# The next image's first q products held in PSUM during a feed-forward, and three smaller moves, in a two-layer attention kernel

## The chip, the cores and the metric

The kernel runs on one core of one Trainium2 chip, as one program. The metric is the device time of one execution in microseconds (us); a kernel's time is the median of its runs. The core's engines each work through an instruction queue of their own in order: TensorE (PE in the profile; PEld are its weight loads), VectorE (DVE), ScalarE (ACT), GpSimd (POOL) and SyncE (SP, which here only issues DMA transfers). They wait for each other through semaphores. Products of PE land in PSUM[...]. The instructions' order within an engine and their waits are laid by a scheduler (the `tile` library) from the Python program; a buffer is taken from a pool, and one that takes the place of an older one waits until that is no longer read.

## The reference

Eight images of 32 x 32 tokens (T = 1024) with C = 384 channels go through two layers, each added to its input. Layer 0 is a group norm and an attention of six heads with a bias from relative positions; layer 1 is a norm and causal attention of one head, and then a norm and a feed-forward with weights cut to signs and activations scaled by their largest absolute value.

```python
# layer 0
qkv = _gn(x).reshape(b, hw, c) @ qkv_w + qkv_b          # -> q, k, v: [48, 1024, 64]
attn = einsum('bqd,bkd->bqk', q * SCALE, k)
rel_h = einsum('bhwc,hkc->bhwk', r_q, Rh); rel_w = einsum('bhwc,wkc->bhwk', r_q, Rw)   # r_q is q, by row and column
attn = softmax(attn + rel_h[..., :, None] + rel_w[..., None, :])
x = x + (attn @ v) @ proj_w + proj_b
# layer 1, attention
t = _ln_t(x);  q, k, v = t @ Wq, t @ Wk, t @ Wv
x = x + softmax(causal(q @ k.T * C ** -0.5)) @ v
# layer 1, feed-forward: sign-cut weights by five groups, activations scaled by absmax per image;
# the groups take in five of eight images: for the other three this part is zero
h = gelu(_bitlinear(_ln_t(x), W1, b1), approximate=False)
x = x + _bitlinear(h, W2, b2)
```

## The kernel before

The kernel works through the images one after the other. PSUM is one pool of eight banks of 128x512 fp32 (`o_tile`); SBUF tiles of 128x1024 are `page` (12 of them), those of 128x3080 `image` or `flat` (11).

The group norm of the next image is made between the value products and the scores of layer 1's attention. Its two small products (mean and variance over the groups, "gmean" and "gvar") each wait for VectorE, and are waited for by it:

```python
def group_norm_T(b, xT=None):
    xT = load_T(b) if xT is None else xT
    ...                                    # bn_stats, bn_aggr -> mv
    nc.tensor.matmul(ps[:, 0:1], over_group, mv[:, 0:1], start=True, stop=True)     # gmean
    nc.vector.tensor_copy(cs[:, 0:1], ps[:, 0:1])
    nc.vector.tensor_tensor(d[:, 0:1], mv[:, 0:1], cs[:, 0:1], ALU.subtract)
    nc.vector.scalar_tensor_tensor(d[:, 1:2], d[:, 0:1], d[:, 0:1], mv[:, 1:2], ALU.mult, ALU.add)
    ps = pools.o_tile(f"gvar_{b}")
    nc.tensor.matmul(ps[:, 0:1], over_group, d[:, 1:2], start=True, stop=True)      # gvar
    ...                                    # sqrt on ScalarE, reciprocal, xT normalized in place
    return xT
```

Layer 0 of an image begins with q and k: for each m (0 to 2 are q of the head pairs, 3 to 5 their k) six products of 128x512. From q come the bias tables ("rel"), which go through DRAM to be laid out anew ("far", "near") and are then split in a rounded part and its rest ("hi" and "lo", by `place`), and sent to the r tiles, hi by SP's queue and lo by POOL's. `place(0, ...)` runs ahead of the bursts; pairs 1 and 2 are fetched step by step from the generator `later`.

```python
def queries_keys(m):
    for half in range(2):
        ps = pools.o_tile(f"qk_{b}_{m}_{half}")
        for i in range(NC):
            nc.tensor.matmul(ps, wqkv_sb[:, i, ts(m, P)], xT[:, i, t], start=(i == 0), stop=(i == NC - 1))
        ...                                # evacuated with the bias added, half 0 by ScalarE, half 1 by VectorE
def place(p, near, pages):
    for d in range(2):
        nc.scalar.copy(hi, src)
        nc.vector.tensor_tensor(lo, src, hi.bitcast(F32), ALU.subtract)
        if d == 0: yield
    for part in range(4):
        for d in range(2):
            for i in range(2):
                (nc.gpsimd if i else nc.sync).dma_start(out=r[part][:, p, :]..., in_=pages[i]...)
for m in range(2 * NPAIR):
    queries_keys(m)
    if 0 < m <= NPAIR:
        near.append(positions(m - 1))      # the rel products, far, near
...                                        # v; place(0) as a whole
if pools.fast and b == 0:
    join_biases(pools)
    multiply_out(pools)                    # wqk = wq @ wk.T * C ** -0.5, once, from wqT and wkT
```

The attention of layer 0 runs in bursts of units. A unit is one block of 128 keys (c) against one half of the queries; its two heads are two products of q and k and two of the unit matrix and r, added in PSUM, and two exponentials. The value products of a burst come behind the scores of the next. `residual` loads x and adds the output bias to it on POOL, eight additions.

```python
for p in range(NPAIR):
    for n, burst in enumerate(bursts):     # 2, 3, 3, 3, 3, 2 units
        prs = [scores(p, *u) for u in burst]
        for u in pending:
            values(*u)
        if n == 0:
            if p > 0: few = set_aside(p - 1, *last)
            elif b > 0: xt = residual()
            avs = ...
        if b == 0 and xt is None and next(signs[0]):   # image 0: a step of the sign-cutting of the weights
            xt = residual()
        if p == 0 and n > 0:
            with tc.issue_after(last_exp[0]):
                next(later, None)          # a step of place for pairs 1 and 2
        ...
```

The feed-forward: a norm in two halves, each with four groups of three transposes ("pt"), twenty-four tiles of the first GEMM (y1) with two evacuations each, the largest absolute value over everything, and only then gelu and the second GEMM (y2).

```python
def ffn(xt, b):
    for half in range(2):
        rs = layer_norm_T(xt, xs[0], half, f"2_{b}", xs[1])
    ...                                    # 24 x 6 products y1, ScalarE evacuates, VectorE takes maxima
    s, _ = absmax_scale(...)               # partition_all_reduce on POOL
    for j in range(NJ):
        ...                                # gelu to hi and lo; 24 products y2; VectorE evacuates
```

Of the kernel before, what the change touches and what calls it, by code (L numbers as in the profile page):

```python
# [17 lines left out]
P = 128  # L18
B, H, W, C = 8, 32, 32, 384
T = H * W  # L20
NJ = T // P
NC = C // P
# [9 lines left out]
B_FFN = NG * GSB  # L32
# [41 lines left out]
def conv_attn_hybrid(  # L74
# [19 lines left out]
    nc = tc.nc  # L94
# [15 lines left out]
    wqkv_sb, wproj_sb, wv_sb = (tile_of(n, [P, NC, w]) for n, w in (("wqkv_sb", 3 * C), ("wproj_sb", C), ("wv_sb", C)))  # L110
# [30 lines left out]
    ident = const.tile([P, P], F32, name="ident")  # L141
# [146 lines left out]

    def stages(pools):

        def transpose_tiles(dst, srcs, engine):

            n = len(srcs)
            pt = pools.o_tile("pt")
            for i, s in enumerate(srcs):
                nc.tensor.transpose(pt[:, ts(i, P)], s, ident)  # L296
            engine(dst, pt[:, : n * P].rearrange("p (i q) -> p i q", i=n))

        def load_T(b):
# [7 lines left out]
        def group_norm_T(b, xT=None):  # L307

            xT = load_T(b) if xT is None else xT
            st = pools.small.tile([P, NC, 2, 6], F32, tag="gst", bufs=2, name=f"gst_{b}")  # L310
            mv = pools.small.tile([P, 2], F32, tag="gmv", name=f"gmv_{b}")
            for k in range(NC):
                for half in range(2):
                    nc.vector.bn_stats(st[:, k, half, :], xT[:, k, ts(half, 512)])
            nc.vector.bn_aggr(mv, st.rearrange("p k a s -> p (k a s)"))

            ps = pools.o_tile(f"gmean_{b}")
            nc.tensor.matmul(ps[:, 0:1], over_group, mv[:, 0:1], start=True, stop=True)
            cs = pools.small.tile([P, 2], F32, tag="gcs", name=f"gcs_{b}")
            nc.vector.tensor_copy(cs[:, 0:1], ps[:, 0:1])  # L320
            d = pools.small.tile([P, 2], F32, tag="gd", name=f"gd_{b}")
            nc.vector.tensor_tensor(d[:, 0:1], mv[:, 0:1], cs[:, 0:1], ALU.subtract)
            nc.vector.scalar_tensor_tensor(d[:, 1:2], d[:, 0:1], d[:, 0:1], mv[:, 1:2], ALU.mult, ALU.add)
            ps = pools.o_tile(f"gvar_{b}")
            nc.tensor.matmul(ps[:, 0:1], over_group, d[:, 1:2], start=True, stop=True)
            nc.vector.tensor_scalar_add(d[:, 0:1], ps[:, 0:1], 1e-5)
            nc.scalar.activation(d[:, 0:1], d[:, 0:1], AF.Sqrt)
            nc.vector.reciprocal(cs[:, 1:2], d[:, 0:1])
            for k in range(NC):
                nc.vector.tensor_scalar(  # L330
                    xT[:, k, :], xT[:, k, :], cs[:, 0:1], cs[:, 1:2], ALU.subtract, ALU.mult
                )
            return xT

        def layer_norm_T(xt, xT, half, name, xlo=None):

# [73 lines left out]
            nc.vector.tensor_reduce(seen[:, 1, i : i + 1], reciprocal, AX.X, ALU.add)  # L410


        def layer0(b, xT):


# [7 lines left out]
            def queries_keys(m):  # L423
                p = m % NPAIR
                bias = bqk[:, m : m + 1]
                for half in range(2):
                    t = ts(half, 512)
                    ps = pools.o_tile(f"qk_{b}_{m}_{half}")
                    for i in range(NC):
                        nc.tensor.matmul(  # L430
                            ps, wqkv_sb[:, i, ts(m, P)], xT[:, i, t], start=(i == 0), stop=(i == NC - 1)
                        )
                    if m < NPAIR:
                        dst = q[:, p, t]
                    else:
                        dst = k[:, p, t].rearrange("d (g n i) -> d g i n", n=2, i=P)
                        ps = ps.rearrange("d (g i n) -> d g i n", n=2, i=P)
                    if half:
                        nc.vector.tensor_scalar_add(dst, ps, bias)
                    else:  # L440
                        nc.scalar.activation(dst, ps, AF.Identity, bias=bias)
# [92 lines left out]
                pass  # L534
            if pools.fast and b == 0:
                join_biases(pools)
                multiply_out(pools)

            def residual():
                xt = load_x(pools, b)  # L540
# [6 lines left out]
        def attend0_fast(residual, b, q, k, r, v, later):  # L547
# [84 lines left out]
            xt = None  # L632
# [6 lines left out]
            for p in range(NPAIR):  # L639
                sums = [pools.page(f"sum0_{b}_{p}_{half}") for half in range(2)]  # L640
                for n, burst in enumerate(bursts):
                    prs = [scores(p, *u) for u in burst]
                    for u in pending:
                        values(*u)
                    if n == 0:
                        if p > 0:
                            few = set_aside(p - 1, *last)
                        elif b > 0:
                            xt = residual()
                        avs = [pools.o_tile(f"av0_{b}_{p}_{half}") for half in range(2)]  # L650
                    if b == 0 and xt is None and next(signs[0]):
                        xt = residual()
                    if p == 0 and n > 0:
                        with tc.issue_after(last_exp[0]):
                            next(later, None)
                    if n == 2 and p > 0:
                        divide(p - 1, few)
                    pending = [(p, *u, pr, sums, avs) for u, pr in zip(burst, prs)]
                last = (sums, avs)
# [71 lines left out]
        def attention1(xt, more, b, between):  # L731
# [29 lines left out]
            for j in range(4, NJ):  # L761
                values(j)

            got = between()
            (attend1_fast if pools.fast else attend1_general)(xt, b, q, xT, v)
            return got

        def attend1_fast(xt, b, q, xT, v):

            room = [pools.flat(f"pr1_{b}_{i}") for i in range(2)]  # L770
            tot = pools.small.tile([P, NJ], F32, tag="tot1", name=f"tot1_{b}")
# [29 lines left out]
            prs = []  # L801
            for c in range(NJ):
                prs.append(scores(c))
                for work in signs:
                    next(work, None)
                if c >= 2:
                    values(c - 2)
# [4 lines left out]
            values(NJ - 1)  # L812
            check(tot, rt, b * (NPAIR + 1) + NPAIR)

        def attend1_general(xt, b, q, xT, v):
            mask = pools.work.tile([P, P], F32, tag="mask", name=f"mask_{b}")
            make_causal_mask(nc, mask, mask_val=MASKED)

# [50 lines left out]
            w2m = [a2[:, ts(i, C)] for i in range(8)] + [rest[:, half + i * C : half + (i + 1) * C] for i in range(4)]  # L869
            return w1k, w2m  # L870

        def ffn(xt, b):
            xs = [pools.halves(f"{n}_{b}", F32R) for n in ("lnT_2", "lnlo_2")]
            for half in range(2):
                rs = layer_norm_T(xt, xs[0], half, f"2_{b}", xs[1])

            early = pools.small.tile([P, 1], F32, tag="early", name=f"early_{b}")
            nc.scalar.activation(early, rs[:, 0:1], AF.Gelu)
# [7 lines left out]
            for half in range(2):  # L886
                for m in range(NM):
# [10 lines left out]
                    if m + 1 in cuts:  # L898
                        n = cuts.index(m + 1)
                        for i in (2 * half, 2 * half + 1):  # L900
                            nc.vector.tensor_reduce(  # L901
                                am[:, i, n - 1 : n], pairs[i][:, cuts[n - 1] : cuts[n], :, :], AX.XYZ, ALU.max, apply_absolute_value=True
                            )
            s, _ = absmax_scale(am.rearrange("p i n -> p (i n)"), f"1_{b}")

# [42 lines left out]
        def run(pools):  # L950
            gn = load_T(0)
            if pools.fast:
                load_weights(pools)
            gn = group_norm_T(0, gn)
            if pools.fast:
                make_unit(pools)
            for b in range(B):
                xt, more = layer0(b, gn)

                def between():  # L960

                    g = group_norm_T(b + 1) if b + 1 < B else None
                    return g

                gn = attention1(xt, more, b, between)
                add = ffn(xt, b) if b < B_FFN else None

                def finish(b=b, xt=xt, add=add):
                    if add:
# [59 lines left out]
```

## Time and profile before

| | |
|---|---|
| Time, median of three runs | 2508.88 us (2507.89 to 2511.79) |
| Span of the profiled execution | 2506.5 us |
| PE clock granted, mean | 0.988 |
| POOL, busy | 300.4 us, 12% |
| q and k products of layer 0 (L430) | 256.9 us, 576 products |
| variance product of image 1's group norm (L325) | begins at 243.11 us, 1.05 us of waiting before it |
| image 0's first feed-forward | from its transposes at 290 us to layer 0 of image 1 at 373.76 us |

The profile's busy share counts an engine as at work from an instruction's start to its modelled end; a PE that is "busy" may still run at half its clock. PEclk in the windows of the trace is the clock that PE was granted, 1.00 being full. A wait is put down to the releaser that came last. Line numbers (L430) are those of the kernel before. A name such as f_qk is the buffer, with f_ for the path of the kernel that runs.

Three stretches of image 0 and 1 around the change, from the windows of the trace (columns: window, length, busy us and instructions of PE, PEld, DVE, ACT, POOL, then PEclk, DMA share, GB/s):

```profile
294.00:296.00 2.00, 0.00 (x0) 0.00 (x0) 0.73 (x2) 1.95 (x4) 0.00 (x0) 0.75 0.00 0
296.00:298.00 2.00, 1.45 (x7) 1.45 (x8) 1.74 (x4) 1.75 (x3) 0.00 (x0) 0.50 0.00 0
298.00:300.00 2.00, 2.00 (x9) 1.84 (x8) 1.75 (x4) 1.44 (x3) 0.00 (x0) 0.50 0.00 0
340.00:342.00 2.00, 2.00 (x8) 2.00 (x7) 0.76 (x2) 1.97 (x3) 0.00 (x0) 0.50 0.00 0
```

They are the end of the second norm, the first products of the feed-forward, and the first products of the second GEMM.

### The profile page before, as it was taken

To read this page: it belongs to the slowest core of one execution; us is meant where nothing else is said; L and a number is where in the kernel's file an instruction comes from. 1 tells how busy PE (TensorE), PEld (TensorE's weight loads), DVE (VectorE), ACT (ScalarE), POOL (GpSimd) and SP (SyncE) were. 2 spreads that over 40 slices of the span, in tenths; PEclk is the share of its full clock that TensorE was granted. 3 is DMA by queue.
4 is the path that set the end of the run, shared out by engine and by line. 5 is a ranking of instruction groups with operands and counts; after the bars stand their busy time and mean duration, and the time that the engine had idled before them with its cause. 6 is when DMAs were issued, how large, how long until landed. Compare 5 with 4: busy or idle time off the path is not lost.

```text
span 2506.5 us, 25716 instructions
## 1 busy us (share of the span) xinstructions
PE 2405.9 (96%) x9378; PEld 1296.8 (52%) x9378; DVE 1416.6 (57%) x2182; ACT 1016.2 (41%) x1742; POOL 300.4 (12%) x389
## 2 busy tenths in 40 slices
PE   7899999999899999999999999989999999999998
PEld 3335684345764456743458544567435543554344
DVE  4696553963556744548645577345585248524852
ACT  3451363631645413645227354145551155114520
POOL 1120002300014000022000230001300031002200
PEclk9999999999999999999999999999999999999999
DMA  7632207211036101082110541011810172007100
GB/s 160 199 119 75 76 1 159 68 64 38 1 86 142 51 13 38 1 179 61 52 38 1 118 109 51 13 38 45 161 48 1 45 144 64 1 26 157 46 0 27
DMA packets 154792, 169.97 MB, mean 68 GB/s; under 512 B 113408, under 2 KB 126048, under 8 KB 153120
## 3 DMA queue, kind: packets, MB, share of 16 engines
q1 hardware_dynamic: 134416, 98.93, 16.9%
q0 software_dynamic: 17184, 69.22, 9.5%
q8 instruction: 77, 1.26, 0.2%
q10 hardware_dynamic: 3056, 0.08, 0.1%
q14 instruction: 59, 0.48, 0.1%
HBM read 75.38 MB, written 42.47 MB: 47 GB/s over the span
## 4 chain that ended last, share of the span: by engine, by line
PE 93%; DVE 2%; DMA 2%; ACT 1%; POOL 1%; issue 1%; SPq 0%; ACTq 0%; DVEq 0%
PE f_s L559 14%; PE f_av L580 14%; PE f_qk L430 10%; PE f_av L794 7%; PE f_s L781 7%; PE f_y L929 7%; PE f_y L890 7%; PE f_v L368 5%; PE f_q L739 5%; PE f_v L507 4%; PE f_s L563 4%; PE f_pj L368 2%; PE f_rel L457 2%; PE f_pj L669 2%; PE f_pt L296 1%; PE f_pj L674 1%
## 5 line engine op out<-in xcount | busy, mean ns | idle before, releaser
L569 ACT ACTIVATE f_pr<-f_s 128x512 f32<-128x512 f32 x768 | 408.5, 597 | 351.5 <-PE f_s L563 294.3
L559 PE MATMUL f_s<-f_q,f_k 64*128 64x512 f32 x1536 | 412.6, 608 | 6.3 <-ACT f_pr L569 6.3
L577 DVE TENSOR_TENSOR f_sum<-f_sum,f_pr 128x1024 f32<-128x1024 f32 x288 | 373.6, 1347 | 17.5 <-ACT f_pr L569 17.0
L580 PE MATMUL f_av<-f_pr,f_v 128*64 128x512 f32 x1536 | 359.6, 601 | 0.0
L563 PE MATMUL f_s<-f_r,unit 64*128 64x512 f32 x768 | 305.8, 767 | 7.8 <-issue 6.7
L430 PE MATMUL f_qk<-f_gnT,wqkv_sb 128*128 128x512 f32 x576 | 256.9, 600 | 2.0 <-DVE f_gnT L330 2.0
L559 PEld LDWEIGHTS f_s<-f_q,f_k 64*128 64x128 f32 x1536 | 145.6, 186 | 173.7 <-issue 98.7
L580 PEld LDWEIGHTS f_av<-f_pr,f_v 128*64 128x64 f32 x1536 | 98.2, 136 | 217.8 <-issue 194.7
L794 PE MATMUL f_av<-f_v,f_pr 128*128 128x385 f32 x576 | 194.5, 486 | 0.0
L781 PE MATMUL f_s<-f_q,f_lnT 128*128 128x512 f32 (+3 forms) x576 | 194.4, 487 | 0.0
L430 PEld LDWEIGHTS f_qk<-f_gnT,wqkv_sb 128*128 128x128 f32 x576 | 108.1, 191 | 144.2 <-issue 131.4
L495 POOL DMA_DIRECT2D f_r<-f_far x192 | 101.8, 533 | 438.8 <-DVE f_far L488 398.1
L794 PEld LDWEIGHTS f_av<-f_v,f_pr 128*128 128x128 f32 x576 | 108.7, 190 | 78.5 <-issue 11.5
L781 PEld LDWEIGHTS f_s<-f_q,f_lnT 128*128 128x128 f32 x576 | 102.6, 190 | 81.0 <-issue 57.4
L788 ACT ACTIVATE f_pr<-f_s 128x512 f32<-128x512 f32 (+3 forms) x96 | 47.1, 490 | 208.8 <-DVE f_s L786 154.3
L563 PEld LDWEIGHTS f_s<-f_r,unit 64*128 64x128 f32 x768 | 79.1, 187 | 101.2 <-issue 99.2
L894 ACT ACTIVATE f_h<-f_y,b_sb 128x256 f32<-128x256 f32 x240 | 99.6, 472 | 72.8 <-PE f_y L890 72.8
L901 DVE TENSOR_REDUCE am<-f_h 128x1 f32<-128x1024 f32 (+2 forms) x80 | 71.6, 946 | 101.5 <-ACT f_h L894 101.5
L739 PE MATMUL f_q<-f_lnT,wqk 128*128 128x512 f32 x288 | 127.5, 592 | 0.0
L368 PE MATMUL f_v<-wv_sb,f_lnT 128*128 128x384 f32 x384 | 126.5, 486 | 0.0
L507 PE MATMUL f_v<-wqkv_sb,f_gnT 128*128 128x384 f32 x384 | 125.1, 486 | 0.0
L542 POOL TENSOR_TENSOR f_x<-f_x,pb 128x384 f32<-128x384 f32 x64 | 117.9, 1871 | 10.0 <-issue 9.7
(161 smaller groups left out, 3015.2 us busy)
## 6 DMA issues: line engine op xcount, KB each, us to landing
f_far<-f_far SPq DMA_DIRECT2D x48, 512.0 KB, 5.2
f_r<-f_far POOLq DMA_DIRECT2D x192, 128.0 KB, 4.1
f_r<-f_far SPq DMA_DIRECT2D x192, 128.0 KB, 2.8
f_gnT<-in_xT SPq DMA_DIRECT2D x24, 512.0 KB, 4.7
f_x<-in_x SPq DMA_DIRECT2D x32, 384.0 KB, 5.4
out_y<-f_x POOLq DMA_DIRECT2D x28, 384.0 KB, 4.3
f_near<-f_far SPq DMA_DIRECT2D x128, 64.0 KB, 4.6
f_w1a<-w1s POOLq DMA_DIRECT2D x5, 1536.0 KB, 6.7
```

Of the source, the lines that this page charges most:

```text
L368: nc.tensor.matmul(ps[:, :C], xT[:, k, ts(j, P)], w[:, k, cols], start=(k == 0), stop=(k == NC - 1))
L430: nc.tensor.matmul(ps, wqkv_sb[:, i, ts(m, P)], xT[:, i, t], start=(i == 0), stop=(i == NC - 1))
L507: nc.tensor.matmul(ps, keys[:, i, j // 2, j % 2], wqkv_sb[:, i, 2 * C :], start=(i == 0), stop=(i == NC - 1))
L559: nc.tensor.matmul(sc[par], k[rows[par], p, ts(c, P)], q[rows[par], p, ts(half, 512)], start=True, stop=False)
L563: nc.tensor.matmul(sc[par], unit[rows[par], c // 2 % 2].rearrange("i h w -> i (h w)"), r[2 * (c // 4) + c % 2][rows[par], p, ts(half, 512) ...
L569: last_exp[0] = nc.scalar.activation(pr[:, ts(par, 512)], sc[par], AF.Exp).ins
L577: nc.vector.tensor_tensor(sums[half], prev, pr, ALU.add)
L580: nc.tensor.matmul(avs[half][ts(par, HD), :], v[:, c, ts(h, HD)], pr[:, ts(par, 512)], start=(c == 0), stop=(c == NJ - 1),)
L739: nc.tensor.matmul(ps, wqk[:, k, ts(m, P)], xT[:, half, k, :], start=(k == 0), stop=(k == NC - 1))
L781: nc.tensor.matmul(sc[:, lo:], xT[:, c // 4, k, ts(c % 4, P)], q[:, half, k, lo:], start=(k == 0), stop=(k == NC - 1),)
L794: nc.tensor.matmul(av[:, : C + 1], prs[c][:, ts(j - c, P)], v[:, c, :], start=(c == 0), stop=(c == j))
L890: nc.tensor.matmul(ps, w1k[i // 2][:, ts(m, P)], xs[i % 2][:, half, i // 2, :], start=(i == 0), stop=(i == 2 * NC - 1))
```

## The change

Four parts, none of which changes what is computed.

1. The q products of layer 0 are split from their evacuation (`project_qk`). While image b's feed-forward runs (images 0 to 4), those of image b + 1 for m = 0 are put behind the last transpose of the norm's first half, and those for m = 1 behind the maximum, ahead of the second GEMM. They stay in PSUM, two banks each, until layer 0's `queries_keys` takes them from the dictionary `ahead` and evacuates them; the scheduler may place the evacuation earlier, as soon as the products are done.
2. `group_norm_T` becomes a generator that pauses before the variance product; it goes on behind the first scores of layer 1's attention.
3. The steps of `place` for pairs 1 and 2 begin with the first burst (`p == 0`) and not the second (`p == 0 and n > 0`), to have r in time for pair 1.
4. `multiply_out`, once a kernel, moves from the place ahead of the bursts to image 0's second burst, so that PE needn't wait there for its two weight loads.

```diff
@@ -288,12 +288,14 @@
 
     def stages(pools):
 
+        last_transpose = [None]
+
         def transpose_tiles(dst, srcs, engine):
 
             n = len(srcs)
             pt = pools.o_tile("pt")
             for i, s in enumerate(srcs):
-                nc.tensor.transpose(pt[:, ts(i, P)], s, ident)
+                last_transpose[0] = nc.tensor.transpose(pt[:, ts(i, P)], s, ident).ins
             engine(dst, pt[:, : n * P].rearrange("p (i q) -> p i q", i=n))
 
         def load_T(b):
@@ -321,6 +323,7 @@
             d = pools.small.tile([P, 2], F32, tag="gd", name=f"gd_{b}")
             nc.vector.tensor_tensor(d[:, 0:1], mv[:, 0:1], cs[:, 0:1], ALU.subtract)
             nc.vector.scalar_tensor_tensor(d[:, 1:2], d[:, 0:1], d[:, 0:1], mv[:, 1:2], ALU.mult, ALU.add)
+            yield xT
             ps = pools.o_tile(f"gvar_{b}")
             nc.tensor.matmul(ps[:, 0:1], over_group, d[:, 1:2], start=True, stop=True)
             nc.vector.tensor_scalar_add(d[:, 0:1], ps[:, 0:1], 1e-5)
@@ -330,7 +333,6 @@
                 nc.vector.tensor_scalar(
                     xT[:, k, :], xT[:, k, :], cs[:, 0:1], cs[:, 1:2], ALU.subtract, ALU.mult
                 )
-            return xT
 
         def layer_norm_T(xt, xT, half, name, xlo=None):
@@ -410,6 +412,18 @@
             nc.vector.tensor_reduce(seen[:, 1, i : i + 1], reciprocal, AX.X, ALU.add)
 
 
+        ahead = {}
+
+        def project_qk(b, xT, m):
+
+            made = [pools.o_tile(f"qk_{b}_{m}_{half}") for half in range(2)]
+            for half in range(2):
+                for i in range(NC):
+                    nc.tensor.matmul(
+                        made[half], wqkv_sb[:, i, ts(m, P)], xT[:, i, ts(half, 512)], start=(i == 0), stop=(i == NC - 1)
+                    )
+            return made
+
         def layer0(b, xT):
@@ -423,13 +437,9 @@
             def queries_keys(m):
                 p = m % NPAIR
                 bias = bqk[:, m : m + 1]
-                for half in range(2):
+                made = ahead.pop((b, m)) if (b, m) in ahead else project_qk(b, xT, m)
+                for half, ps in enumerate(made):
                     t = ts(half, 512)
-                    ps = pools.o_tile(f"qk_{b}_{m}_{half}")
-                    for i in range(NC):
-                        nc.tensor.matmul(
-                            ps, wqkv_sb[:, i, ts(m, P)], xT[:, i, t], start=(i == 0), stop=(i == NC - 1)
-                        )
                     if m < NPAIR:
                         dst = q[:, p, t]
                     else:
@@ -534,7 +544,6 @@
                 pass
             if pools.fast and b == 0:
                 join_biases(pools)
-                multiply_out(pools)
 
             def residual():
                 xt = load_x(pools, b)
@@ -640,6 +649,8 @@
                 sums = [pools.page(f"sum0_{b}_{p}_{half}") for half in range(2)]
                 for n, burst in enumerate(bursts):
                     prs = [scores(p, *u) for u in burst]
+                    if b == 0 and (p, n) == (0, 1):
+                        multiply_out(pools)
                     for u in pending:
                         values(*u)
                     if n == 0:
@@ -650,7 +661,7 @@
                         avs = [pools.o_tile(f"av0_{b}_{p}_{half}") for half in range(2)]
                     if b == 0 and xt is None and next(signs[0]):
                         xt = residual()
-                    if p == 0 and n > 0:
+                    if p == 0:
                         with tc.issue_after(last_exp[0]):
                             next(later, None)
                     if n == 2 and p > 0:
@@ -761,11 +772,12 @@
             for j in range(4, NJ):
                 values(j)
 
-            got = between()
-            (attend1_fast if pools.fast else attend1_general)(xt, b, q, xT, v)
+            room = between()
+            got = next(room, None)
+            (attend1_fast if pools.fast else attend1_general)(xt, b, q, xT, v, room)
             return got
 
-        def attend1_fast(xt, b, q, xT, v):
+        def attend1_fast(xt, b, q, xT, v, other):
 
             room = [pools.flat(f"pr1_{b}_{i}") for i in range(2)]
             tot = pools.small.tile([P, NJ], F32, tag="tot1", name=f"tot1_{b}")
@@ -801,6 +813,7 @@
             prs = []
             for c in range(NJ):
                 prs.append(scores(c))
+                next(other, None)
                 for work in signs:
                     next(work, None)
                 if c >= 2:
@@ -869,10 +883,14 @@
             w2m = [a2[:, ts(i, C)] for i in range(8)] + [rest[:, half + i * C : half + (i + 1) * C] for i in range(4)]
             return w1k, w2m
 
-        def ffn(xt, b):
+        def ffn(xt, b, gn):
             xs = [pools.halves(f"{n}_{b}", F32R) for n in ("lnT_2", "lnlo_2")]
             for half in range(2):
                 rs = layer_norm_T(xt, xs[0], half, f"2_{b}", xs[1])
+
+                if half == 0 and gn is not None and pools.fast:
+                    with tc.issue_after(last_transpose[0]):
+                        ahead[b + 1, 0] = project_qk(b + 1, gn, 0)
 
             early = pools.small.tile([P, 1], F32, tag="early", name=f"early_{b}")
             nc.scalar.activation(early, rs[:, 0:1], AF.Gelu)
@@ -902,6 +920,8 @@
                                 am[:, i, n - 1 : n], pairs[i][:, cuts[n - 1] : cuts[n], :, :], AX.XYZ, ALU.max, apply_absolute_value=True
                             )
             s, _ = absmax_scale(am.rearrange("p i n -> p (i n)"), f"1_{b}")
+            if gn is not None and pools.fast:
+                ahead[b + 1, 1] = project_qk(b + 1, gn, 1)
@@ -959,11 +980,11 @@
 
                 def between():
 
-                    g = group_norm_T(b + 1) if b + 1 < B else None
-                    return g
+                    if b + 1 < B:
+                        yield from group_norm_T(b + 1)
 
                 gn = attention1(xt, more, b, between)
-                add = ffn(xt, b) if b < B_FFN else None
+                add = ffn(xt, b, gn) if b < B_FFN else None
 
                 def finish(b=b, xt=xt, add=add):
                     if add:
```

(Cut: the same pause for the general path that does not run here, and the consumption of the generator for image 0, `for _ in group_norm_T(0, gn): pass`.)

## The prediction

> **What bounds the kernel now.** I read the page first: the engines' busy time, then the chain that ended last.
>
> ```profile
> PE 2405.9 (96%) x9378; PEld 1296.8 (52%) x9378; DVE 1416.6 (57%) x2182; ACT 1016.2 (41%) x1742; POOL 300.4 (12%) x389
> ...
> PE 93%; DVE 2%; DMA 2%; ACT 1%; POOL 1%; issue 1%; SPq 0%; ACTq 0%; DVEq 0%
> ```
>
> TensorE works through 96% of the span and makes 93% of the chain. The change removes no product: it can only fill or remove the hundred microseconds in which PE stands still, or runs slowly after standing still. So the second view is the list of PE's waits (engine, line, releaser; total us, times, longest).
>
> ```profile
> PE f_pt L296 <- DVE xn L358: 26.8, 18, 2.8
> PE f_y L929 <- ACT f_hi L914: 19.4, 9, 3.7
> PE f_gmean L318 <- DVE gmv L315: 10.9, 1, 10.9
> PE f_wqk L286 <- DMA f_wqkT<-in_wkT: 10.1, 1, 10.1
> PE f_gvar L325 <- DVE gd L323: 8.0, 8, 1.1
> PE f_s L563 <- issue: 6.7, 6, 1.3
> PE f_s L559 <- ACT f_pr L569: 6.3, 14, 0.5
> ```
>
> The change aims at five of these rows: f_pt, f_y, f_wqk, f_gvar and the six f_s. The third view is PE's timeline of image 0's norm and feed-forward and of image 1's start (start, us, operation; in brackets the idle time before it).
>
> ```profile
> 293.22 0.52 PE L296 MATMUL f_pt<-ident,xn 128*128 128x128 f32 x3 [2.06 <-DVE xn L358]
> 296.55 2.83 PE L296 MATMUL f_pt<-ident,xn 128*128 128x128 f32 x12 [2.81 <-DVE xn L358]
> 299.02 0.78 PE L890 MATMUL f_y<-f_lnT,f_w1a 128*128 128x512 f32 x1
> ...
> 337.74 0.79 PE L929 MATMUL f_y<-f_w2a,f_hi 128*128 128x384 f32 x3 [3.67 <-ACT f_hi L914]
> ...
> 373.76 10.46 PE L430 MATMUL f_qk<-f_gnT,wqkv_sb 128*128 128x512 f32 x24
> 384.15 1.99 PE L457 MATMUL f_rel<-f_q,rel 64*128 64x512 f32 x8
> ```
>
> There are three gaps per feed-forward (2.06, 2.81, 3.67), and at 373.76 a block of 24 q products, 10.39 us up to the next operation, that depend only on data ready long before. Twelve of them (one m) take 5.2 us.
>
> [...] PEclk is 0.75 in the window 294 to 296 and 0.50 in 296 to 300 and in 340 to 342; the transposes behind the 2.81 gap take 2.47 us where the same twelve take 1.45 warm, and the first feed-forward products come every 0.43 us instead of 0.23. A filled gap thus gives back more than its length. [...] A q product of 128x512 fills one; holding 2 for m = 0 and 2 for m = 1 leaves 4 to the feed-forward. The 6.3 us of f_s <- f_pr show that PE does wait for banks in the bursts; no trace yet shows it in the feed-forward. [...] POOL's r transfers take a median of 4.1 from issue to landing, which I use.
>
> **The change part by part**, as after minus before.
>
> *1. Next image's q products in norm and feed-forward (5 images).* It removes 10.39 us at the start of layer 0. Half of it, m = 0, goes behind the last transpose of the norm's first half, into the 2.81 gap. The gap goes, but 5.2 is longer than it: the feed-forward starts 5.2 - 2.81 - 1.0 (transposes now warm) = 1.4 to 1.6 us later. Then the first products, no longer slow, give back 0.8 (lost in images 0 to 4: 1.35, 0.33, 1.7, 0.5, 0.23, counted as the slow products times 0.20). The net cost is 0.8, so 5.2 - 0.8 = 4.4 is saved. The other half, m = 1, goes into the 3.67 gap before the second GEMM. Before, from the end of the last y1 (334.07) to the end of the first 24 y2 products (344.40) were 10.33 us, the products slow (6.66). After: 5.35 + 4.22 warm = 9.57. So the block costs less than nothing: 5.2 + 0.76, minus 0.3 for two evacuations of 0.69 us that the scheduler puts among ScalarE's gelus = 5.7. Sum: 10.1 a feed-forward, times 5 = -50. At the start of layer 0 the rel products then follow at once; q was evacuated long before, and 4 rel + 2 held banks fit in 8, so I expect no new wait.
>
> *2. Variance of the group norm behind the first scores (7 images).* The matmul no longer waits for DVE: 8.0 less the one of image 0 = -7.3. ScalarE loads a table twice more per image, 1.28 us each, with ScalarE at 41%: hidden.
>
> *3. Casts of the bias tiles one burst earlier.* Before, pair 1's first bias product waits for its r transfers, 1.1 to 1.3 us in 7 images, 7.8 in all. These waits go. But see the order of POOL, which issues half of the transfers and makes the eight residual adds:
>
> ```profile
> 441.04 0.53 POOL L495 DMA_DIRECT2D f_r<-f_far  x1 [19.45 <-DVE f_far L488]
> 441.59 3.09 POOL L542 TENSOR_TENSOR f_x<-f_x,pb 128x384 f32<-128x384 f32 x2
> 444.63 0.55 POOL L495 DMA_DIRECT2D f_r<-f_far  x1
> 445.20 11.79 POOL L542 TENSOR_TENSOR f_x<-f_x,pb 128x384 f32<-128x384 f32 x6
> 456.93 3.17 POOL L495 DMA_DIRECT2D f_r<-f_far  x6
> ```
>
> The instruction order of the changed kernel still has the last r transfers behind the eight adds, and its buffer allocation now gives the page of pair 1's lo tile to the probabilities of pair 0's unit (6,1), where before it went to pair 1's first unit. So an exponential waits for those transfers. Second cast ends on ScalarE near 440.5, on VectorE near 442; then 0.5 + 3.1 + 0.5 + 11.8 + about 0.6 of issues gives a last issue near 458 and a landing of 4.1 later, 462. The exponential was due at 452.5; its value product, due on PE at 459.3, would start near 462.7. That is 3.4 of new stall against 1.1 removed: +2.3 an image, 7 images: +16 if it happens so, -7.8 if not. I give it two in three: 0.67 x 16 - 0.33 x 7.8 = +8.
>
> *4. wq @ wk.T among image 0's bursts.* Its 10.1 us wait for the transposed weights goes, and its products, slow after the wait (8.61 for 18), would take 5.9. Against that, POOL's weight loads for the sign sums, before at 64.5, now stand behind pair 1's r transfers (near 84), so they land near 92. VectorE's evacuations of the three wqk banks stand behind sums that need those loads, and PE's scores of the next burst need these banks: I make it 11 us of stall until about 97 to 102. Net 0 to +2.
>
> Sum: -50 - 7 + 8 + 1 = -48, or 2508.9 - 48 = 2461.
>
> **The rivals.** *A, every wait goes and nothing takes its place:* -50 - 7.3 - 7.8 - about 8 for part 4 = -73, 2436. For it: transfers may be issued earlier than I place them, and the allocation has slack elsewhere. Against it: the order of POOL and of VectorE. *B, waits change their names (mine in full):* -50 - 7 + 16 + 2 = -39, 2470. For it: in-order queues on POOL and VectorE. *C, the held banks starve the feed-forward:* with 4 or 6 banks instead of 8, y1's products would wait for ScalarE's two evacuations (0.47 each, L894). ScalarE is idle before them for 72.8 us in total, so it keeps pace, and two banks in turn cover it; I give it little. It would halve part 1: about 2486. *D, the cushion:* the 10 us of q products before also hid the DVE and DMA work behind the start of layer 0. If the rel evacuations or the r transfers of pair 0 come late, 2 to 4 us an image come back: up to 2480.
>
> **Range and chances.** Part 1 is the firmest, two thirds or more of it nearly sure. The range runs from near A, 2438, to B plus half of D, 2480. Faster by 2% means below 2459, almost on my number: 0.46, within 2% 0.51, slower 0.03.
>
> **What would show it.** In the changed profile: f_pt at most one wait of 2 us a feed-forward (some 10 left of 26.8), f_y near 0 to 4, no 0.50 clock between transposes and first products, f_rel straight at layer 0's start with no wait over 1 us (step 1). No f_gvar wait, f_gmean unchanged (2). No f_s <- r wait but a row f_av <- ACT f_pr, some 7 times up to 3.4, with ScalarE's exponential waiting for an f_r transfer (3). No wqk <- DMA wait, but f_s waiting on VectorE's wqk or sums around 85 to 102 (4). I am wrong if y1 waits for banks, if f_rel or the first bias products wait at the start of layer 0, or if neither of the stalls of 3 and 4 is there.

## The result, and the profile after

The changed kernel takes 2480.86 us (median of four runs, 2479.12 to 2482.41) against 2509.52 before in the same comparison: a ratio of 0.9885, 95% interval 0.9868 to 0.9902. That is 28.7 us or 1.14% less. The prediction had 48 us less, and its range ended at 2480.

First the engines' busy time and the chain that ended last, from the page of the changed kernel.

```profile
PE 2407.4 (97%) x9378; PEld 1285.8 (52%) x9378; DVE 1418.0 (57%) x2182; ACT 1032.1 (42%) x1756; POOL 287.1 (12%) x389
...
PE 89%; POOL 4%; DVE 2%; DMA 2%; issue 1%; ACT 1%; SPq 0%; ACTq 0%; DVEq 0%; POOLq 0%
```

The products are the same 9378. What is new is POOL in the chain: 4% where before it had 1%. An engine that is busy for 12% of the span now sets the pace at some places. The list of PE's waits in the changed kernel says where (line numbers shift by some ten: 568 and 572 are the products of f_s, 589 the value products of layer 0):

```profile
PE f_av L589 <- ACT f_pr L578: 16.3, 6, 2.8
PE f_pt L298 <- DVE xn L360: 12.7, 13, 2.1
PE f_gmean L320 <- DVE gmv L317: 11.3, 1, 11.3
PE f_s L568 <- DVE wqk L287: 11.0, 1, 11.0
PE f_s L568 <- ACT f_pr L578: 9.2, 16, 2.5
PE f_bad L196 <- DVE worst L194: 1.8, 1, 1.8
PE f_qk L422 <- DVE f_gnT L333: 1.6, 1, 1.6
PE f_gvar L328 <- DVE gd L325: 0.7, 1, 0.7
```

The rows the change aimed at are gone or halved: f_y from 19.4 to none, f_pt from 26.8 to 12.7, f_wqk from 10.1 to none, f_gvar from 8.0 to 0.7, the six f_s L563 to none. Three rows are new or larger: f_av waiting for an exponential (16.3, six times), f_s for VectorE's wqk (11.0, once), and f_s for exponentials (9.2 against 6.3; 2.5 of it is image 6's stall, which shows at f_s and not at f_av).

Waits alone don't give the time. I cut both traces at the same three products of each image: the last value projection (v) of layer 0, the last value product (av) of layer 0, and the last one of layer 1. The sums of these stretches, in us of the profiled executions:

| Stretch | before | after | difference |
|---|---|---|---|
| image 0: bursts of layer 0 | 120.5 | 127.2 | +6.7 |
| images 1 to 7: bursts of layer 0 | 724.2 | 746.2 | +22.0 |
| all: projection, norm and attention of layer 1 | 799.7 | 791.2 | -8.5 |
| images 0 to 4: feed-forward, and next image's q, k, v | 677.7 | 631.0 | -46.7 |
| the rest (start, images 5 and 6 to the next bursts, end) | 184.6 | 184.1 | -0.5 |
| Span | 2506.5 | 2479.7 | -26.8 |

So two parts of the change brought 55 us, and the other two cost 29.

The gains are as intended. From PE's timeline of the changed kernel, image 0's second norm, second GEMM, and start of layer 0 of image 1:

```profile
298.25 0.52 PE L298 MATMUL f_pt<-ident,xn 128*128 128x128 f32 x3 [2.06 <-DVE xn L360]
298.60 5.32 PE L422 MATMUL f_qk<-f_gnT,wqkv_sb 128*128 128x512 f32 x12
303.75 1.50 PE L298 MATMUL f_pt<-ident,xn 128*128 128x128 f32 x11
...
338.64 5.31 PE L422 MATMUL f_qk<-f_gnT,wqkv_sb 128*128 128x512 f32 x12
343.39 1.61 PE L949 MATMUL f_y<-f_w2a,f_hi 128*128 128x384 f32 x6
...
378.00 1.99 PE L467 MATMUL f_rel<-f_q,rel 64*128 64x512 f32 x8
379.92 5.42 PE L422 MATMUL f_qk<-f_gnT,wqkv_sb 128*128 128x512 f32 x12
```

The q products stand where there was a gap, the transposes and the second GEMM follow without waiting, and layer 0 begins with f_rel at once. No product of the feed-forward and no f_rel of images 1 to 5 waits for a bank.

The 22 us lie in the first pair of heads of images 1 to 7. Image 1, in the changed kernel, first POOL's timeline:

```profile
436.56 0.53 POOL L505 DMA_DIRECT2D f_r<-f_far  x1 [3.19 <-DVE f_far L498]
437.12 3.23 POOL L551 TENSOR_TENSOR f_x<-f_x,pb 128x384 f32<-128x384 f32 x2
440.29 0.55 POOL L505 DMA_DIRECT2D f_r<-f_far  x1
440.86 11.16 POOL L551 TENSOR_TENSOR f_x<-f_x,pb 128x384 f32<-128x384 f32 x6
451.96 3.18 POOL L505 DMA_DIRECT2D f_r<-f_far  x6
```

Then ScalarE's and PE's, one line each:

```profile
455.29 3.04 ACT L578 ACTIVATE f_pr<-f_s 128x512 f32<-128x512 f32 x6 [8.92 <-DMA f_r<-f_far]
```

```profile
455.94 1.56 PE L589 MATMUL f_av<-f_pr,f_v 128*64 128x512 f32 x4 [2.67 <-ACT f_pr L578]
```

Read upwards: PE waits 2.67 us for an exponential; ScalarE had waited 8.92 us to write it, as the page it writes was still being read by r transfers; these stood on POOL behind the eight residual adds until 451.96. This is the stall that the prediction's part 3 describes.

The 6.7 us of image 0 lie in one place too. PE, then VectorE, then POOL:

```profile
98.94 1.22 PE L568 MATMUL f_s<-f_q,f_k 64*128 64x512 f32 x1 [11.05 <-DVE wqk L287]
```

```profile
94.07 4.35 DVE L234 TENSOR_REDUCE sums_w<-f_w 128x1 f32<-128x614 f32 x7 [9.15 <-DMA f_w<-in_w1T]
98.34 0.55 DVE L287 TENSOR_SCALAR wqk<-f_wqk 128x384 f32<-128x384 f32 x1
...
102.29 0.55 DVE L287 TENSOR_SCALAR wqk<-f_wqk 128x384 f32<-128x384 f32 x1
```

```profile
79.61 3.68 POOL L505 DMA_DIRECT2D f_r<-f_far  x7 [17.64 <-DVE f_far L498]
83.28 1.30 POOL L227 DMA_DIRECT2D f_w<-in_w1T  x2
```

POOL stands for 17.64 us at an r transfer of pair 1, whose cast isn't done; the weight loads behind it go out at 83.28 (before: 64.52). VectorE waits 9.15 us for them, with the evacuations of wqk behind. PE waits 11.05 us for the first of the three banks and then runs at the pace of the other two and at half clock (PEclk 0.50 from 92.64) until 109.7.

### The profile page after: what moved, and what is told of

Read it like the earlier page. It is cut to its first block, busy times and chain, and to the rows that moved or that the text cites. A ratio compares the mean times of both kernels' runs of the same rounds, so it can differ in the third digit from the quotient of the medians.

```text
span 2479.7 us, 25709 instructions
## 1 busy us (share of the span) xinstructions
PE 2407.4 (97%) x9378; PEld 1285.8 (52%) x9378; DVE 1418.0 (57%) x2182; ACT 1032.1 (42%) x1756; POOL 287.1 (12%) x389
## 4 chain that ended last, share of the span: by engine, by line
PE 89%; POOL 4%; DVE 2%; DMA 2%; issue 1%; ACT 1%; SPq 0%; ACTq 0%; DVEq 0%; POOLq 0%
PE f_s L568 12%; PE f_av L589 11%; PE f_qk L422 10%; PE f_s L793 8%; PE f_av L806 8%; PE f_y L949 7%; PE f_y L908 7%; PE f_v L370 5%; PE f_v L517 5%; PE f_q L750 5%; POOL f_x L551 3%; PE f_s L572 3%; PE f_pj L370 2%; PE f_rel L467 2%; PE f_pj L680 2%
## 5 line engine op out<-in xcount | busy, mean ns | idle before, releaser
L568 PE MATMUL f_s<-f_q,f_k 64*128 64x512 f32 x1536 | 422.4, 616 | 20.3 <-DVE wqk L287 11.0
L589 PE MATMUL f_av<-f_pr,f_v 128*64 128x512 f32 x1536 | 368.7, 608 | 16.3 <-ACT f_pr L578 16.3
L586 DVE TENSOR_TENSOR f_sum<-f_sum,f_pr 128x1024 f32<-128x1024 f32 x288 | 368.3, 1329 | 17.2 <-ACT f_pr L578 16.9
L572 PE MATMUL f_s<-f_r,unit 64*128 64x512 f32 x768 | 312.2, 777 | 0.0
L422 PE MATMUL f_qk<-f_gnT,wqkv_sb 128*128 128x512 f32 x576 | 262.1, 609 | 1.6 <-DVE f_gnT L333 1.6
L806 PEld LDWEIGHTS f_av<-f_v,f_pr 128*128 128x128 f32 x576 | 108.6, 190 | 78.6 <-issue 11.5
L912 ACT ACTIVATE f_h<-f_y,b_sb 128x256 f32<-128x256 f32 x240 | 100.9, 472 | 68.4 <-PE f_y L908 68.4
L750 PE MATMUL f_q<-f_lnT,wqk 128*128 128x512 f32 x288 | 127.5, 592 | 0.0
L517 PE MATMUL f_v<-wqkv_sb,f_gnT 128*128 128x384 f32 x384 | 125.2, 486 | 0.0
L551 POOL TENSOR_TENSOR f_x<-f_x,pb 128x384 f32<-128x384 f32 x64 | 107.2, 1705 | 18.4 <-DMA f_x<-in_x 18.1
```

Source lines behind the costliest of these rows:

```text
L422: nc.tensor.matmul(made[half], wqkv_sb[:, i, ts(m, P)], xT[:, i, ts(half, 512)], start=(i == 0), stop=(i == NC - 1))
L517: nc.tensor.matmul(ps, keys[:, i, j // 2, j % 2], wqkv_sb[:, i, 2 * C :], start=(i == 0), stop=(i == NC - 1))
L551: nc.gpsimd.tensor_tensor(xt[:, j, :], xt[:, j, :], pb, ALU.add)
L568: nc.tensor.matmul(sc[par], k[rows[par], p, ts(c, P)], q[rows[par], p, ts(half, 512)], start=True, stop=False)
L572: nc.tensor.matmul(sc[par], unit[rows[par], c // 2 % 2].rearrange("i h w -> i (h w)"), r[2 * (c // 4) + c % 2][rows[par], p, ts(half, 512) ...
L586: nc.vector.tensor_tensor(sums[half], prev, pr, ALU.add)
```

## The experiments

Theory W: the early casts (part 3) are what costs. In images 1 to 7 they bring POOL's order and a reused page to bear on the exponentials; in image 0 they hold back the weight loads. Rivals: G, the bursts are longer because layer 0 lost its cushion of q products; S, image 0's loss comes from the place of wq @ wk.T; Q, POOL's DMA queue as such is the cause. The stretches of the table above, for all kernels (us, from one trace each; time and ratio from the timed runs, each against the kernel before on the same chip, 2511 to 2513 us):

| Kernel | image 0 | bursts 1 to 7 | feed-forward, 5 | time | ratio (95% interval) |
|---|---|---|---|---|---|
| late_casts | 118.4 | 724.1 | 625.9 | 2449.02 | 0.9750 (0.9737 to 0.9763) |
| wqk_back | 121.6 | 745.1 | 634.1 | 2475.78 | 0.9854 (0.9839 to 0.9869) |
| lo_by_sp | 123.1 | 714.6 | 632.6 | 2450.83 | 0.9759 (0.9745 to 0.9772) |
| wqk_by_act | 126.6 | 741.8 | 634.3 | 2478.95 | 0.9863 (0.9848 to 0.9878) |
| adds_later | 127.5 | 714.6 | 632.7 | 2452.52 | 0.9763 (0.9749 to 0.9776) |
| before_early_casts | 122.9 | 749.9 | 676.4 | 2534.07 | 1.0088 (1.0075 to 1.0102) |
| late_m0 | 118.6 | 724.4 | 654.5 | 2475.85 | 0.9858 (0.9843 to 0.9873) |
| late_m1 | 117.4 | 724.1 | 651.8 | 2471.78 | 0.9838 (0.9825 to 0.9852) |
| split_by_image | 118.6 | 714.7 | 634.3 | 2442.08 | 0.9718 (0.9704 to 0.9731) |
| split_wqk_later | 129.3 | 714.6 | 631.0 | 2453.60 | 0.9765 (0.9752 to 0.9779) |
| split_loads_early | 114.6 | 714.6 | 630.6 | 2439.25 | 0.9720 (0.9706 to 0.9733) |

**late_casts**, the changed kernel without part 3:

```diff
-                    if p == 0:
+                    if p == 0 and n > 0:
                         with tc.issue_after(last_exp[0]):
                             next(later, None)
```

> The changed kernel with part 3 undone: the casts of pairs 1 and 2 begin with the second burst again. Theory W (waits took the place of the removed ones: early casts make pair 0's exponential of unit (6,1) wait for r transfers that stand behind the residual adds on POOL, and in image 0 put POOL's weight loads behind pair 1's r transfers): the bursts of images 1 to 7, 22.0 us longer in all than before, fall back to the length of before, and in image 0 the 11 us stall and the 17 us at half clock after it go, as the weight loads are issued near 64.5 us again: 2480.9 - 22 - 15 to 19 = 2440 to 2444. Rival G (the bursts are longer because the start of layer 0 has lost its cushion of q products, casts innocent): within 5 us of 2480.9. Rival S (image 0's loss comes from the new place of wq @ wk.T alone): 2459, image 0 unchanged.

One line undone makes the kernel 32 us faster. The bursts are at 724.1, the length of before, and the waits of f_av are gone; G is out, as the cushion is still missing here. In image 0 POOL's loads go out at 65.67 again, and 8.8 us are won, half of what I had expected: the loads of wq and wk are late again (5.4 us) and the slow products behind them too (7.86 us for the 18 of wqk). The two sets of loads seem to stand in each other's way. In late_casts those of wq and wk are issued at 70.39 and 71.03, behind POOL's first weight loads, and take 12.9 and 13.8 us to land. In the kernel before, with the same order, they take 12.7 and 13.3, the DMA engines fully busy (share 1.03 from 70 to 77 us); in the changed kernel, where they are issued at 65.2 and 65.8 ahead of POOL's, 4.4 and 5.3. PE's waits in late_casts, the rows that matter:

```profile
PE f_pt L298 <- DVE xn L360: 12.7, 13, 2.1
...
PE f_s L568 <- ACT f_pr L578: 6.8, 15, 0.5
PE f_s L572 <- issue: 6.5, 6, 1.1
PE f_wqk L286 <- DMA f_wqkT<-in_wkT: 5.4, 1, 5.4
```

The six waits of f_s for pair 1's r, which part 3 was meant to remove, are back with 6.5 us. Removing them is worth 9.5 us in the bursts (724.1 here, 714.6 in lo_by_sp and adds_later below); the stall that part 3 brings along costs 31.6 (746.2 against the same 714.6).

**before_early_casts**, the kernel before with part 3 alone:

```diff
-                    if p == 0 and n > 0:
+                    if p == 0:
```

> The kernel before with part 3 alone, the early casts. Theory W: that part alone makes the kernel slower: the seven bursts 724.2 to about 745, image 0 about 1 us longer (as in wqk_back, 121.6 against 120.5): 2512 + 22 = 2534. If the stall needs the held banks or the shorter start of layer 0 (rival G), the early casts alone win their 7.8 us: 2504.

2534.07: as theory W has it, and the sign of the effect without any other part of the change. The agreement to the microsecond is in part luck, as the bursts took 749.9 us in the trace and not 745. The wait is the same one:

```profile
PE f_av L580 <- ACT f_pr L569: 16.8, 6, 2.9
```

**lo_by_sp**, all four parts, with another queue for the lo transfers:

```diff
-                            (nc.gpsimd if i else nc.sync).dma_start(
+                            (nc.gpsimd if i and p == 0 else nc.sync).dma_start(
                                 out=r[part][:, p, :]...
```

> The changed kernel, all four parts, but the lo transfers of pairs 1 and 2 are issued by SyncE and not by POOL, so that they stand behind no residual add and POOL's weight loads stand behind no r transfer. Theory W: both stalls go and the 7.8 us wait for pair 1's r stays away: 2480.9 - 22 - 7.8 - 15 to 19 = 2432 to 2436. Rival G: no change, 2476 to 2483. A new wait of its own is possible: SyncE's queue issues twice as many r transfers, and hi ones may stand behind lo ones that wait for VectorE.

The bursts do what was expected, 746.2 to 714.6: the stall is gone and pair 1's wait stays away. Image 0 gained 4.1 us only, not 15 to 19, and the time is 15 to 19 us above what was expected. POOL's weight loads begin at 64.70 here, on time, and yet image 0 takes 123.1 us against 118.4 in late_casts; VectorE waits 6.39 us for the last of these loads, against 3.91 there. So some 5 us of image 0's loss don't come from POOL's order. Whether the early casts as such or SyncE's longer queue costs them wasn't tested.

**adds_later** leaves the transfers on POOL and moves the adds:

```diff
-                        elif b > 0:
-                            xt = residual()
...
+                    if b > 0 and (p, n) == (0, 3):
+                        xt = residual()
```

> The changed kernel, lo transfers still issued by POOL, but from image 1 on the residual adds come three bursts later in the program, so that pair 1's r transfers stand ahead of them on POOL. If the order on POOL is the cause (theory W) and not the queue itself, the bursts of images 1 to 7 become as short as with SyncE, 714.6 us, image 0 stays at 127: 2480.9 - 31.6 = 2449. Rival Q (POOL's DMA queue is slower than SyncE's, or early casts alone bring the stall): bursts stay near 746, 2481.

714.6 again, to the tenth, with POOL's queue: it is the order on POOL and not the queue; Q is out. POOL's timeline in adds_later, image 1:

```profile
437.86 2.11 POOL L505 DMA_DIRECT2D f_r<-f_far  x4 [3.22 <-DVE f_far L498]
442.52 2.11 POOL L505 DMA_DIRECT2D f_r<-f_far  x4 [2.55 <-DVE f_far L498]
447.64 8.70 POOL L551 TENSOR_TENSOR f_x<-f_x,pb 128x384 f32<-128x384 f32 x4 [3.01 <-DMA f_x<-in_x]
```

All of pair 1's transfers are issued by 444.6; in the changed kernel the last of them came after 451.96. Image 0 keeps its 127.5, as nothing was done there.

**wqk_back** undoes part 4:

```diff
                     prs = [scores(p, *u) for u in burst]
-                    if b == 0 and (p, n) == (0, 1):
-                        multiply_out(pools)
...
                 join_biases(pools)
+                multiply_out(pools)
```

> The changed kernel with part 4 undone: wq @ wk.T ahead of the bursts again, casts early. Theory W: image 0's bursts fall back by what they had gained, 6.7 us, to 2474, with the 10 us wait for the transposed weights back and no wait of f_s for VectorE's wqk; bursts of images 1 to 7 as in the changed kernel, six or seven stalls of 2.7. Rival S says the same of the time. If early casts alone harm image 0 (POOL's loads late, then the cut of the signs late), it stays within 3 of 2480.9.

Image 0 falls from 127.2 to 121.6, the time to 2475.78. With part 3 in place, part 4 loses 5.6 in image 0; without it (late_casts, 118.4 against 120.5 before) it wins 2. So S is half true: the new place is harmful only together with the late weight loads. And the early casts don't make these loads late by themselves. POOL's timeline in wqk_back has the first one on time:

```profile
63.93 0.75 POOL L227 DMA_DIRECT2D f_w<-in_w1T  x1
```

In before_early_casts it is at 65.31. Only the kernels with parts 3 and 4 together and the lo transfers on POOL have it at 83 to 85 (changed kernel, adds_later, wqk_by_act). In image 0 it is the pair of parts, and POOL's order that follows from it, that holds back the loads; why the scheduler lays that order wasn't tested.

**wqk_by_act** takes the evacuations out of VectorE's queue:

```diff
-            nc.vector.tensor_scalar_mul(wqk[:, m, :], ps[:, :C], C**-0.5)
+            nc.scalar.mul(wqk[:, m, :], ps[:, :C], C**-0.5)
```

> The changed kernel, but the three products of wq @ wk.T are evacuated by ScalarE and not by VectorE, whose queue holds the sums of late weights ahead of them. Theory W: the 11 us wait of f_s for wqk and the half clock after it go, the rest stays: 2480.9 - 15 to 19 = 2462 to 2466. If the evacuation is not what holds the banks (the sums' lateness itself delays the bursts), within 3 of 2480.9.

My expectation failed: 126.6 in image 0, hardly a gain. The wait for the banks went and two others came, in image 0 of wqk_by_act (f_den are the small products that sum up the exponentials of a head pair, from VectorE's "few"):

```profile
PE f_den L621 <- DVE few L613: 7.7, 1, 7.7
PE f_s L568 <- ACT f_pr L578: 5.2, 2, 4.7
```

It is the lateness of the weights that holds VectorE, and through it PE at the next thing VectorE has to do. The held banks were only the first place where it showed. late_casts, which has the loads early, is the repair as far as it goes (8.8 us).

**late_m0 and late_m1** measure the two halves of part 1, each against late_casts:

```diff
# late_m0: late_casts without
-                ahead[b + 1, 1] = project_qk(b + 1, gn, 1)
# late_m1: late_casts without
-                        ahead[b + 1, 0] = project_qk(b + 1, gn, 0)
```

> The kernel of late_casts (2449.0) with only m = 0 of the next image's q products ahead, in the norm's gap; m = 1 is made at the start of layer 0 again. By the prediction's sizes m = 1 was worth 5.7 us a feed-forward: 2449.0 + 5 x 5.7 = 2477.5, the wait f_y <- f_hi back at 19.4. If the gap ahead of the second GEMM alone counts and no cold products (3.9 an image): 2468.5.

> The kernel of late_casts with only m = 1 ahead, before the second GEMM; m = 0 at the start of layer 0 again. By the prediction's sizes m = 0 was worth 4.4 us a feed-forward: 2449.0 + 5 x 4.4 = 2471, the f_pt row back near 26.8. If the block in the norm mostly moves the first GEMM back and saves only its gap (2.8): 2463.

m = 1 is worth 2475.85 - 2449.02 = 26.8, or 5.4 a feed-forward (predicted 5.7); m = 0 is worth 22.8, or 4.6 (predicted 4.4). The kernel before differs by 1.0 us between the two comparisons, so each may be 0.2 less. Each takes its own row of waits away. In late_m0:

```profile
PE f_y L947 <- ACT f_hi L932: 18.7, 6, 3.7
PE f_pt L298 <- DVE xn L360: 12.7, 13, 2.1
```

In late_m1 it is f_pt alone that is back:

```profile
PE f_pt L298 <- DVE xn L360: 26.8, 18, 2.8
```

More is won than the gaps (2.8 and 3.7) are long: the rest is work that no longer runs slowly behind them. The feed-forward stretches of late_m0's trace have seven times 3.41 us at half clock and those of late_m1's ten times; late_casts' have none (mean granted clock 0.993, 0.991 and 0.998).

**split_by_image** puts the two repairs together, each where it is needed:

```diff
-                            (nc.gpsimd if i else nc.sync).dma_start(
+                            (nc.gpsimd if i and (p == 0 or b == 0) else nc.sync).dma_start(
...
-                    if p == 0:
+                    if p == 0 and (b > 0 or n > 0):
```

> All four parts, but in image 0 the casts start with the second burst and POOL issues lo, as in late_casts, and from image 1 on the casts start with the first burst and SyncE issues the lo transfers of pairs 1 and 2, as in lo_by_sp. The two repairs touch different images, so theory W expects their sum: image 0 as in late_casts (118.4 us from its values to the last value product of layer 0), the seven bursts as in lo_by_sp (714.6): 2449.0 - 9.5 = 2439.5. Rival: what lo_by_sp won in the bursts it loses elsewhere (its feed-forwards took 6.7 us more): 2446.

2442.08, about 39 us faster than the changed kernel. Image 0 and the bursts are those of the two parents, as expected; the feed-forwards took 634.3 in the profiled execution against 625.9 in late_casts, of which more below.

**split_wqk_later** and **split_loads_early** try to end what remains of image 0's wait for the loads of wq and wk. The first moves products and loads one burst on (`(p, n) == (0, 2)` in place of `(0, 1)`). The second splits them:

```diff
+            if pools.fast and b == 0:
+                loaded.append(load_wqkT(pools))        # only the two transfers
             for _ in place(0, *near[0]):
                 pass
...
-                        multiply_out(pools)
+                        multiply_out(pools, *loaded.pop())     # only the products
```

> split_by_image with wq @ wk.T one burst later, in the third. In late_casts the second of its two loads landed 5.4 us after PE had come to it, and its products then ran partly at half clock (7.86 for 18 instead of 5.9 us). A burst, about 7 us, covers this: 5.4 + 1 to 2 less than split_by_image, 2432 to 2433. If the loads start later too, or VectorE's queue in that burst holds the banks, no gain.

> split_by_image (2442.1) with the two loads of wq @ wk.T issued ahead of pair 0's r transfers, and only the products in the second burst. The wait of wqk for its loads (5.0 us) and the half clock behind it (1.7) go: 2435 to 2437. If the loads delay pair 0's r transfers, by sharing the DMA engines or SyncE's queue, the start of image 0's bursts gives it back: 2441 to 2446.

The later burst cost 11.5 us: the loads moved along with the products (issued at 85.21, against 68.12 in split_by_image), so that 4.1 of the wait of 5.0 stayed, and VectorE, with more ahead of it, added 6.4. PE's waits in split_wqk_later:

```profile
PE f_s L568 <- DVE seen L411: 6.4, 1, 6.4
PE f_wqk L286 <- DMA f_wqkT<-in_wkT: 4.1, 1, 4.1
```

The earlier loads won 4 us in image 0's trace (114.6), and a 4.2 us wait for VectorE took the place of the 5.0 for the loads:

```profile
PE f_den L627 <- DVE few L619: 4.2, 1, 4.2
```

In the median that is 2439.25 against 2442.08, two intervals that overlap, so the last step isn't shown beyond the trace. Both are the fastest kernels here, 2.8% under the kernel before.

## Why the prediction was wrong

**Part 1, -50: right.** Measured -46.7 in the traces, and 4.6 and 5.4 for the two halves against 4.4 and 5.7. The missing 3 to 5 us are three stretches of 3.41 us at half clock, 1.7 us lost in each, in the norms of images 1 to 3, behind the 2.06 gap that the prediction let stand. late_casts has none of them and shows -51.8; its trace is of the fastest of its five runs. Rivals C (banks) and D (cushion) didn't happen: no y1 product waits, f_rel begins at once.

**Part 2, -7: right.** -8.5, in every kernel with this part (791.2 against 799.7).

**Part 3, +8: this step failed.** Measured +22.0. The mechanism was the one described, order on POOL, page, exponential, value product, with the last r issues at 451.96 and later in a stretch that began 6 us earlier than before, so the same place. Two terms were wrong. First, a stall that I had read from the instruction order of the changed kernel was taken at two thirds, and a gain of 7.8 at one third mixed in: 16 became 8. (The seven waits behind the 7.8 were 0.9 to 1.3 us, not 1.1 to 1.3; their sum is right.) Second, the stall itself was sized without the clock. It is 2.7 us and not 3.4, and in images 1 to 3 the burst stretch is 1.9 to 2.1 longer, close to the predicted 2.3. In images 4 to 7 it is 3.6 to 4.9, because the stall there is followed by one or two stretches of 3.4 us at half clock (from 1451.15, 1782.24, 2031.41 and 2301.07). I had counted the clock as a gain where gaps go, and not as a loss where new ones come.

**Part 4, +1: this step failed too, in its size.** Measured +6.7, together with part 3's casts in image 0. The stall was predicted at 11 us and is 11.05. What follows it was left out: the second and third banks came free only at 100.9 and 102.8, and PE ran at half clock until 109.7. By the stretch up to the start of the fourth burst (+6.8 = 11.05 + 0.45 new waits, less 10.09 of wait and 2.54 of slow wqk products, plus the rest), the rest is 8.0 us.

The sum: -46.7 - 8.5 + 22.0 + 6.7 - 0.5 = -27, where I had -50 - 7 + 8 + 1 = -48. Of the rivals B, with 2470, was the nearest in mechanism: what it lacks is in the main the half clock, behind the new stalls and in the norms. C (2486) and the end of D (2480) are nearer in number, but neither y1 nor the start of layer 0 waited, so that is chance. The range ended at 2480 for the same reason: its upper end had room for a cushion effect that didn't come, and none for this.

## What to carry to other kernels

Work put into a gap of the engine that bounds the kernel was worth the gap and the slow work behind it (5.4 us for a gap of 3.7, 4.6 for one of 2.8), and could be sized from one timeline. Before something is started earlier, look at the in-order queues it will stand in (here GpSimd's adds and loads) and at who next takes the buffer it holds: a transfer that was late but harmless became a wait of the bound engine, and one line gave back about half of what the other parts had won. Size a new stall with the clock it costs (here 3.4 or 6.8 us at half clock behind the stalls of 2.5 to 2.8 in images 4 to 7), and when a wait moves as one link is taken away (f_s for wqk, then f_den), look for the link that all of them share.

## What the runs showed of the hardware

The stretches at half clock don't begin where a gap ends. In image 0's norm the kernel before has one from 294.99, within the gap that ends at 296.55; in image 1's norm the changed kernel has one from 628.53, 0.6 us behind the gap. The kernel before has 11 of them in its trace and the changed kernel 8 (the one that the program's end cuts off left out). They last 3.41 us, or two, three or five times as long (6.83, 10.24 and 17.07), and within a trace their starts lie whole multiples of 3.41 us apart (628.53, 959.63 and 1290.72 in the changed kernel: 97 times 3.413 from one to the next).

The same gap is followed by half clock in one image and not in the other. The norm in two images of the changed kernel, in stretches of 3.41 us (stretch, length, busy us and instructions of PE, PEld, DVE, ACT, POOL, then PEclk, DMA share, GB/s), image 1 first:

```profile
625.09:628.50 3.41, 1.35 (x12) 1.13 (x11) 3.31 (x10) 1.26 (x4) 0.00 (x0) 1.00 0.00 0
628.50:631.91 3.41, 3.41 (x5) 1.35 (x4) 2.08 (x6) 3.35 (x5) 0.00 (x0) 0.51 0.00 0
631.91:635.32 3.41, 3.41 (x10) 1.46 (x9) 0.08 (x1) 0.09 (x1) 0.00 (x0) 0.99 0.00 0
```

and image 0:

```profile
293.99:297.41 3.42, 2.20 (x13) 1.42 (x11) 2.13 (x8) 1.24 (x3) 0.00 (x0) 1.00 0.27 104
297.41:300.82 3.41, 2.57 (x9) 1.41 (x10) 2.07 (x6) 1.97 (x4) 0.00 (x0) 1.00 0.02 5
```

The gap is 2.06 us in both. In image 1 it lies in one of these stretches, PE is busy in it for 1.35 of 3.41 us, and the next runs at half clock (PEclk 0.51); in image 0 it is split between two, PE is busy for 2.20 and 2.57 us, and PEclk stays at 1.00. What decides between the two isn't shown. So half clock can follow a gap of 2.06 us, and doesn't follow each such gap.

In the changed kernel a feed-forward stretch takes 125.3 and 125.2 us in images 0 and 4 and 126.8 to 126.9 in images 1 to 3, which have one such half-clock stretch each; the five together take 625.9 to 634.3 over the kernels that share them. As the edits of these kernels don't touch the feed-forward, I put that down to how many of its norms have one, at 1.7 us each; that is an estimate from the changed kernel's five and isn't shown for the others. It may also be why the five times of split_by_image spread over 7 us: the fastest, 2439.03, had a mean granted clock of 0.998, the other four 0.995.
